# Layer-norm tiles of 32 rows from each quarter of a group of 512

## The chip, the core and the metric

The kernel runs on one core of one Trainium2 chip. A core has five engines, each with its own queue of instructions in a fixed order: TensorE (PE) for matmuls, VectorE (DVE) and ScalarE (ACT) for elementwise work, GpSimd (POOL) for elementwise work and for issuing some DMA transfers, and SyncE (SP), which here only issues DMA transfers. Engines wait for one another through semaphores. Sixteen DMA engines move the data. The metric is the device time of one execution in microseconds (us).

## What is computed

The input x has 2 batches of 1,024 tokens with 512 features. Four blocks follow one another, each adding its result to x:

```python
x = x + attn_a(layernorm(x))     # gated linear attention, 4 heads, chunks of 128 tokens, a state per head
x = x + ffn(layernorm(x))        # silu(gate) * up, down; integer weights with scales, 1408 hidden
x = x + attn_b(layernorm(x))     # softmax attention over the 1,024 tokens of a batch
x = x + ffn(layernorm(x))        # the same ffn again

def layernorm(x, eps=1e-05):
    m = mean(x, axis=-1); v = var(x, axis=-1)
    return (x - m) / sqrt(v + eps)
```

A layer norm works on each token by itself. What follows it is a product over the 512 features, so the normed tile is needed turned, with features on the partitions and tokens along the row.

## The kernel before

The 2,048 tokens are 16 tiles of 128 rows (`NT`). Four tiles (`ST`) are a group of 512, and there are four groups (`NST`). The stages are called a (first attention), f (first ffn), b (second attention) and g (second ffn). Between the stages x lies in DRAM, as x1 behind a, x2 behind f and x3 behind b, each as 16 tensors of 128 rows. x1 is stored at L680 and x2 at L931.

Matrices are kept as a high and a low part, and a product is made of three matmuls (L89, L90, L91) or, in the f and g stages and for the scores of b, as seven products of combined 2x2 blocks instead of eight (L338, L1023). ACT makes the high part (L75), DVE the low one (L76). Nearly all of TensorE's time goes to these.

The layer norm of 14 of the 16 group norms goes the way that the change touches: groups 2 and 3 of a, and all four groups of f, b and g. (Groups 0 and 1 of a are turned by TensorE, `ln_tile`, L130.) `ln_steps` gives eight steps for a group, four of `ln_norm` and four of `ln_move`:

- `ln_norm` loads a tile of 128 rows to a buffer `xin` (L102, on SP; two buffers, and the next tile is asked for together with the present one), takes mean and variance on DVE (`bn`, L109, `mv`, L111), adds eps and takes the power -1/2 on POOL (`ve`, L113, `rs`, L115, and for a and f also L119), and writes the normed tile `xn`, on ACT for a and f (L120), on DVE for b and g (L122). DVE then turns it in blocks of 32x32 into `y` (L198), whose layout on a partition is (b, k, i, q): b for the block of 32 features within 128, k for the 128 features, i for the tile in the group, q for the token in its block of 32. There is one `y` buffer, so the next group's turn waits for the moves of this one.
- `ln_move` moves the blocks to the right partitions, to `xT` (L209): for each b and each c (block of 32 tokens in the tile) one DMA from 32 partitions to 32 partitions, 16 in a group. The token of a column of `xT` is 128 i + 32 c + q, so for given c a partition's data is 16 pieces of 32 floats: 128 bytes each, 512 pieces to a move. SP issues the moves of a and f, of b0, b1 and g3, and half of b2; POOL issues the others, 72 of 224.

Later steps split `xT` in high and low parts (`xh`, `xl`, `ln_split`) or combine two groups first (`combine`, L257).

Where these steps stand is set by two things. The program hands them out by tables (in a, the table `fill` gives the tile at which each step is written), and a scheduler then orders every engine's instructions by a timeline of its own, under the dependencies and under extra ones that the program states with `behind`. In a, `q_head` (L91, `pq`), `kv_tile` (`pWk`, `pWv`, evicted as `sWk`, `sWv` at L571), `k_norm` (squares at L588), `scores` (`pS`, L650, from `kT`, L624, and `qT`, L519) and `chunk_out` (`pl`, `pg`; `xra` at L669 and L677; the state at L644) run for one tile after another, with the decay rows (`row`, L534, L545) made by POOL and ACT. A dependency through a DRAM tensor goes by that tensor: a load waits for the stores to the tensor it reads.

Of the kernel before, what the change touches and what calls it, by code (L numbers as in the profile page):

```python
# [9 lines left out]
F32 = mybir.dt.float32  # L10
# [6 lines left out]
P = 128  # L17
D = 512
# [3 lines left out]
NT = NB * T // P  # L22
# [3 lines left out]
ST = 4  # L26
NST = NT // ST
# [7 lines left out]
def hybrid_block_kernel(ctx: ExitStack, tc: tile.TileContext, a, out):  # L35
    nc = tc.nc
# [7 lines left out]
    dp = ctx.enter_context(tc.tile_pool(name="dram", bufs=1, space=bass.MemoryType.DRAM))  # L44
# [55 lines left out]
    def load_x(src, name, tag="xin"):  # L100
        xin = (rp if tag == "xres" else xp).tile([P, D], F32, tag=tag, name=f"xin_{name}")
        nc.sync.dma_start(out=xin, in_=src)  # L102
        return xin
# [31 lines left out]

    bq_s, sg_s, su_s = cols[:, 0:H], cols[:, H : H + KH], cols[:, H + KH : H + 2 * KH]

    x_in = a["x"]
    x1 = [dp.tile([P, D], F32, tag=f"x1_{t}", name=f"x1_{t}") for t in range(NT)]
    x2 = [dp.tile([P, D], F32, tag=f"x2_{t}", name=f"x2_{t}") for t in range(NT)]  # L140
    x3 = [dp.tile([P, D], F32, tag=f"x3_{t}", name=f"x3_{t}") for t in range(NT)]
    cl_d = [dp.tile([16, P], F32, tag=f"cl_{g}", name=f"cl_{g}") for g in range(NST)]
    p_d = [dp.tile([T // P, P, P], F32, tag=f"p_{i}", name=f"p_{i}") for i in range(NC)]
    vo_d = [dp.tile([P, 1024], F32, tag=f"vo_{k}", name=f"vo_{k}") for k in range(KD)]
# [41 lines left out]
    lnT, lnY, lnX, laid = {}, {}, {}, []  # L186

    def ln_norm(src, nm, st, i):


        t = st * ST + i
        for n in range(t, min(t + 2, st * ST + ST)):
            if (nm, n) not in lnX:
                lnX[nm, n] = load_x(src[n], f"{nm}{n}")
        if i == 0:
            lnY[nm, st] = yp.tile([P, 4, KD, ST, 32], F32, tag="y", name=f"y_{nm}{st}")
        xn = layernorm(lnX[nm, t], f"{nm}{t}", by_act=nm in "af")
        done = nc.vector.transpose(lnY[nm, st][:, :, :, i, :], xn.rearrange("p (k b q) -> p b k q", k=KD, b=4))  # L198
        laid[:] = [done.ins]

    def ln_move(nm, st, b):

        if b == 0:
            lnT[nm, st] = slot(f"xT_{nm}{st}").rearrange("p (k c) -> p k c", k=KD)
        y = lnY[nm, st]
        xf = lnT[nm, st].bitcast(F32).rearrange("p k (i b q) -> p (k i) b q", i=ST, b=4)
        for c in range(4):
            sync = nm in "af" or (nm, st) in (("b", 0), ("b", 1), ("g", 3)) or ((nm, st) == ("b", 2) and c % 2)
            (nc.sync if sync else nc.gpsimd).dma_start(  # L209
                out=xf[32 * b : 32 * (b + 1), :, c, :],  # L210
                in_=y[32 * c : 32 * (c + 1), b].rearrange("p k i q -> p (k i) q"),
            )

    def ln_split(nm, st):
# [10 lines left out]
    def ln_steps(src, nm, st):  # L225

        return [lambda i=i: ln_norm(src, nm, st, i) for i in range(ST)] + [
            lambda b=b: ln_move(nm, st, b) for b in range(4)
        ]
# [118 lines left out]
    with ExitStack() as actx:  # L348
# [11 lines left out]
            out=le, in_=ones, compare_op=ALU.is_ge, fill=0.0, base=0, pattern=[[1, P]], channel_multiplier=-1  # L360
# [9 lines left out]
        rows = a1.tile([P, 2 * D + 96], F32, name="rows")  # L370
# [38 lines left out]
                    done.extend(split(w[:, 0:512], w[:, 512:1024], staged[:, k]))  # L409
            return load if staged is None else done  # L410

        xa = [x_in[t * P : (t + 1) * P, :] for t in range(NT)]

        def ln_tile(t):
            st, i = divmod(t, ST)
# [315 lines left out]

        fill = [[] for _ in range(NT)]
        for src, nm, g, its in (
            (xa, "a", 2, (0, 0, 0, 1, 1, 1, 1, 1)),
            (xa, "a", 3, (2, 2, 3, 4, 4, 5, 5, 5)),
            (x1, "f", 0, (6, 6, 7, 7, 7, 7, 8, 8)),
            (x1, "f", 1, (9, 9, 10, 10, 10, 10, 11, 11)),
        ):
            for t, step in zip(its, ln_steps(src, nm, g)):
                fill[t].append(step)  # L740
# [6 lines left out]
        moving = combine("f", 0)  # L747
        wcs, loads = [], []
# [59 lines left out]
    def ffn(src, dst, nm, wcs, moving, ended, after):  # L808
# [3 lines left out]
        with ExitStack() as fctx:  # L812
# [5 lines left out]
            for pr in range(2):  # L818
# [90 lines left out]
                for i in range(2 * ST):  # L909
                    t = pr * 2 * ST + i  # L910
                    if 1 <= i < 2 * ST - 2:
                        n = i + 2
                        for js in (slice(0, 6), slice(6, KH)):
                            done = h_split(n, js, ha[:, n - 2, js] if n < ST else hb[:, n - ST, js], None)
                    xr = rp.tile([P, D], F32, tag="xres", name=f"xr{nm}{t}")
                    with behind((half,)):
                        nc.sync.dma_start(out=xr, in_=src[t])
                    o = fp.tile([P, 512], F32, tag="sg", name=f"o{nm}{t}")

                    last = nm == "g" and t == NT - 1  # L920
                    for ds in [slice(0, 256), slice(256, 512)] if last else [slice(0, 512)]:
                        ps = psum(f"po{nm}{t}_{ds.start}")[:, ds]
                        for j in range(KH):
                            nc.tensor.matmul(ps, hs[i][0][:, j], wd[j][:, ds], start=j == 0, stop=False)  # L924
                            nc.tensor.matmul(ps, hs[i][1][:, j], wd[j][:, ds], start=False, stop=j == KH - 1)  # L925
                        nc.vector.tensor_tensor(o[:, ds], ps, sd_b[:, ds], ALU.mult)
                        nc.vector.tensor_tensor(xr[:, ds], o[:, ds], xr[:, ds], ALU.add)
                        if last:
                            nc.sync.dma_start(out=dst[t][:, ds], in_=xr[:, ds])
                    if not last:  # L930
                        nc.sync.dma_start(out=dst[t], in_=xr)  # L931
                    with behind(done):
                        for _ in range((0, 3, 3, 2, 2, 2, 2, 0)[i]):
                            if early or late:
                                (early or late).pop(0)()
                    if pr == 0 and i in (3, 5, 6):
                        wcs.append(stationary(len(wcs), f"{nm}1", queue=nc.gpsimd))

    of_b = combine("b", 0)
    ffn(  # L940
        x1,
        x2,
        "f",
        wcs,
        moving,
        spilled,
        (ln_steps(x2, "b", 0) + ln_steps(x2, "b", 1), of_b[:6]),
    )


# [2 lines left out]
    with ExitStack() as bctx:  # L953
# [245 lines left out]
        wvo = blocks(vo_d, "wvo0_")  # L1199
        moving = of_b[6:]  # L1200
        for b in range(NB):
            nm, src, g = ("b", x2, 2) if b == 0 else ("g", x3, 0)
            norm = ln_steps(src, nm, g) + ln_steps(src, nm, g + 1)
            if b == 0:
                for kt in (4, 5, 6, 7):
                    array(v_tile, 0, kt)
                do(moving, 6)
                wm = blocks(m_d, "wm")
                do(norm, 8)
                for kt in range(4):  # L1210
                    array(v_tile, 0, kt)
                array(q_proj, 0, 0, range(KD))
            else:
                do(moving, 1)
                array(out_b, 0, 5)
                array(q_proj, 1, 0, range(KD))
                for i in (6, 7):
                    probs_split(0, i, last)
                do(moving, 4)
                array(out_b, 0, 6)  # L1220
                do(norm, 2)
                array(out_b, 0, 7)
                wvo = blocks(vo_d, "wvo1_")
                for kt in (4, 5, 6, 7):
                    array(v_tile, 1, kt)
                do(moving, 2)
                for kt in range(4):
                    array(v_tile, 1, kt)
                do(norm, 2)
                do(moving, 4)  # L1230
                do(norm, 4)
            q_operands(b, 0, False)
            q_operands(b, 0, True)
            if b == 0:
                do(norm, 2)
            cycle(b, 0, lambda: q_proj(b, 1, (0, 1)))
            for i in (0, 1):
                probs_T(b, i)
            do(norm, 2)
            cycle(b, 1, lambda: q_proj(b, 1, (2, 3)))  # L1240
            for i in (2, 3):
                probs_T(b, i)
            do(norm, 4 if b == 0 else 6)
            array(out_b, b, 0)
            if b:
                moving = combine("g", 0)
            cycle(b, 2, lambda: out_b(b, 1))
            for i in (4, 5):
                probs_T(b, i)
            array(out_b, b, 2)  # L1250
            if b == 0:
                moving = combine("b", 1)
                do(moving, 1)

            def between():
                out_b(b, 3)
                if b:
                    with behind(summed):
                        do(moving, 2)

            cycle(b, 3, between)
            if b == 0:
                for i in (6, 7):
                    probs_T(b, i)
                array(out_b, b, 4)
# [9 lines left out]
        ended = (array(out_b, 1, 7),)  # L1275

    out_t = [out[t * P : (t + 1) * P, :] for t in range(NT)]
    ffn(x3, out_t, "g", wcs, moving, ended, ([], []))


# [60 lines left out]
```

## Time and profile before

| | |
|---|---|
| runs | 927.61, 927.32, 926.01 us |
| median | 927.32 us |
| the profiled execution | 926.9 us |
| its span, from first to last instruction | 925.2 us |
| granted TensorE clock | 1.00 |
| DMA | 216,182 packets, 162.20 MB; 151,024 packets under 512 bytes |
| hardware queue (SP's transfers) | 212,624 packets, 53.7% of 16 engines' time |

The stages follow one another in time, with overlaps. Busy time in stretches of the span, in us:

| stretch | length | PE | DVE | ACT | POOL | DMA share |
|---|---|---|---|---|---|---|
| 0 to 100 (a) | 100 | 98.17 | 63.85 | 55.63 | 44.12 | 0.61 |
| 100 to 225 (a) | 125 | 124.60 | 83.40 | 70.75 | 60.62 | 0.61 |
| 225 to 420 (f) | 195 | 195.00 | 164.18 | 102.00 | 59.09 | 0.68 |
| 420 to 530 (f, b) | 110 | 110.00 | 86.80 | 44.62 | 25.10 | 0.56 |
| 530 to 690 (b) | 160 | 159.20 | 123.67 | 66.67 | 30.05 | 0.60 |
| 690 to 925 (g) | 235 | 231.49 | 168.53 | 94.23 | 38.44 | 0.48 |

A row of the groups in the profile reads: line, engine, operation, output<-input, count; then for one view the shortest, median and longest duration in ns, for another the start and duration in us with the idle time ahead of it and what ended it. A row "engine line <- engine line: a, n, c" says that the first waited for the second a us in all, n times, at most c us. The time from a DMA's issue to its landing is given apart from the time that the issue itself takes.

### The profile page before, as it was taken

What the parts mean: (1) busy time and instruction counts of PE and PEld (TensorE: products, weight loads), DVE (VectorE), ACT (ScalarE), POOL (GpSimd) and SP (SyncE); (2) the same over time, 40 slices, a digit from 0 to 9 for tenths busy, and PEclk for the clock granted to TensorE, in tenths of its full rate; (3) what the DMA queues carried; (4) which work ended last, traced back from release to release, by engine and by line L of the source; (5) the groups of instructions that cost most, each with busy time, mean ns of one, the idle gap of its engine ahead of it and who ended that gap; (6) DMA issues with size and microseconds to landing.
All of it is one profiled execution on the core that took longest, in us unless ns stands there. A gap on an engine that the chain in (4) does not pass through costs nothing.

```text
span 925.2 us, 13659 instructions
## 1 busy us (share of the span) xinstructions
PE 918.5 (99%) x4546; PEld 778.1 (84%) x4546; DVE 690.4 (75%) x1335; ACT 433.9 (47%) x928; POOL 257.4 (28%) x458
## 2 busy tenths in 40 slices
PE   9999999999999999999999999999999999999998
PEld 7899999998888888888888888888878888888887
DVE  6755657479998798778848878569968886967654
ACT  5645365556776334444234444145434444344431
POOL 4345334557563002211130401140501631001100
PEclk9999999999999999999999999999999999999999
DMA  9535655477979754724733769225969735454022
GB/s 304 210 100 124 208 160 152 158 207 262 367 236 321 214 178 153 216 47 150 281 82 83 171 168 261 69 45 137 239 140 369 259 126 137 165 205 138 22 69 80
DMA packets 216182, 162.20 MB, mean 175 GB/s; under 512 B 151024, under 2 KB 167728, under 8 KB 216112
## 3 DMA queue, kind: packets, MB, share of 16 engines
q1 hardware_dynamic: 212624, 150.05, 53.7%
q0 software_dynamic: 3488, 11.28, 4.5%
q8 instruction: 36, 0.59, 0.3%
q14 instruction: 34, 0.28, 0.1%
HBM read 104.76 MB, written 41.84 MB: 158 GB/s over the span
## 4 chain that ended last, share of the span: by engine, by line
PE 94%; DVE 2%; SPq 1%; DMA 1%; issue 1%; ACT 0%; POOL 0%; DVEq 0%; ACTq 0%
PE pXf L338 4%; PE pog L925 4%; PE pog L924 4%; PE pZf L338 4%; PE pof L925 4%; PE pXg L338 4%; PE pVg L338 4%; PE pVf L338 4%; PE pZg L338 4%; PE pof L924 4%; PE pob L91 3%; PE pob L89 3%; PE pob L90 3%; PE psZ L1023 2%; PE psX L1023 2%; PE psV L1023 2%
## 5 line engine op out<-in xcount | busy, mean ns | idle before, releaser
L924 PE MATMUL pog<-wdg,hsg 128*128 128x512 f32 (+1 forms) x165 | 60.1, 375 | 0.0
L925 PE MATMUL pog<-wdg,hsg 128*128 128x512 f32 (+1 forms) x165 | 60.0, 375 | 0.0
L925 PE MATMUL pof<-wdf,hsf 128*128 128x512 f32 x154 | 59.1, 389 | 0.0
L924 PE MATMUL pof<-wdf,hsf 128*128 128x512 f32 x154 | 58.9, 389 | 0.0
L91 PE MATMUL pob<-vh,ptl 128*128 128x512 f32 x128 | 49.9, 390 | 0.8 <-DVE ptl L76 0.8
L89 PE MATMUL pob<-vh,pth 128*128 128x512 f32 x128 | 49.9, 390 | 0.0
L90 PE MATMUL pob<-vl,pth 128*128 128x512 f32 x128 | 49.8, 389 | 0.0
L76 POOL TENSOR_TENSOR hsg<-sgg,hsg 128x128 fp32r<-128x128 f32 x40 | 18.9, 491 | 110.4 <-ACT hsg L75 102.6
L338 PE MATMUL pXg<-B_g,wcg 128*128 128x512 f32 x176 | 46.2, 389 | 0.0
L338 PE MATMUL pVf<-T_f,wcf 128*128 128x512 f32 x176 | 46.2, 389 | 0.0
L338 PE MATMUL pVg<-T_g,wcg 128*128 128x512 f32 x176 | 46.2, 389 | 0.0
L338 PE MATMUL pXf<-B_f,wcf 128*128 128x512 f32 x176 | 45.9, 390 | 0.0
L113 POOL TENSOR_SCALAR ve_g<-mv_g 128x1 f32<-128x1 f32 x16 | 7.7, 486 | 129.6 <-DVE mv_g L111 129.6
L209 POOL DMA_DIRECT2D xT_g<-y_g x48 | 31.1, 655 | 38.5 <-DVE T_b L76 29.2
L338 PEld LDWEIGHTS pXf<-B_f,wcf 128*128 128x128 f32 x176 | 32.9, 188 | 7.1 <-issue 0.3
L338 PEld LDWEIGHTS pVf<-T_f,wcf 128*128 128x128 f32 x176 | 33.0, 188 | 6.9
L338 PEld LDWEIGHTS pVg<-T_g,wcg 128*128 128x128 f32 x176 | 33.0, 188 | 6.9
L338 PEld LDWEIGHTS pXg<-B_g,wcg 128*128 128x128 f32 x176 | 33.0, 188 | 6.9
L545 ACT ACTIVATE row<-row,ncl 128x128 f32<-128x128 f32 x64 | 20.5, 391 | 35.4 <-POOL row L534 35.4
L113 POOL TENSOR_SCALAR ve_b<-mv_b 128x1 f32<-128x1 f32 x16 | 5.7, 359 | 112.4 <-DVE mv_b L111 112.2
L924 PEld LDWEIGHTS pog<-wdg,hsg 128*128 128x128 f32 x165 | 31.1, 188 | 5.7
L925 PEld LDWEIGHTS pog<-wdg,hsg 128*128 128x128 f32 x165 | 31.0, 188 | 5.6
(344 smaller groups left out, 2837.4 us busy)
## 6 DMA issues: line engine op xcount, KB each, us to landing
wcg<-wc SPq DMA_DIRECT2D x19, 896.0 KB, 5.0
wc<-wcf SPq DMA_DIRECT2D x11, 896.0 KB, 5.8
p<-py SPq DMA_DIRECT2D x15, 512.0 KB, 3.5
wcf<-wc SPq DMA_DIRECT2D x8, 896.0 KB, 6.3
ptl<-p SPq DMA_DIRECT2D x56, 128.0 KB, 3.1
xin_a<-in_x SPq DMA_DIRECT2D x16, 256.0 KB, 5.3
xra<-in_x SPq DMA_DIRECT2D x16, 256.0 KB, 3.4
row<-cl SPq DMA_DIRECT2D x16, 256.0 KB, 4.3
```

Of the source, the lines that this page charges most:

```text
L76: return c.ins, (eng or nc.vector).tensor_tensor(lo, src, hi.bitcast(F32), ALU.subtract).ins
L89: nc.tensor.matmul(ps, lhs_hi, rhs_hi, start=first, stop=False)
L90: nc.tensor.matmul(ps, lhs_hi, rhs_lo, start=False, stop=False)
L91: end = nc.tensor.matmul(ps, lhs_lo, rhs_hi, start=False, stop=last).ins
L113: nc.gpsimd.tensor_scalar(ve, mv[:, 1:2], EPS, None, ALU.add)
L209: (nc.sync if sync else nc.gpsimd).dma_start(out=xf[32 * b : 32 * (b + 1), :, c, :], in_=y[32 * c : 32 * (c + 1), b].rearrange("p k i q -> ...
L338: nc.tensor.matmul(ps, w[:, m, k * P : (k + 1) * P], o[:, s, k, :], start=first and k == 0 and s == 0, stop=k == 1 and s == 1, skip_group_ ...
L545: nc.scalar.activation(row[:, h, :], row[:, h, :], AF.Exp, bias=ncl[:, n : n + 1], scale=-1.0)
L924: nc.tensor.matmul(ps, hs[i][0][:, j], wd[j][:, ds], start=j == 0, stop=False)
L925: nc.tensor.matmul(ps, hs[i][1][:, j], wd[j][:, ds], start=False, stop=j == KH - 1)
L1023: ends[nm] = nc.tensor.matmul(ps, o[:, i, k], w[:, j, k], start=first and k == 0 and i + j == 0, stop=k == 1 and i == 1, skip_group_check= ...
```

## The change

x1, x2 and x3 become four tensors of 512 rows each; `in_tiles` gives the old tiles of 128 rows as slices of them, for the stores and for the residual loads. A layer-norm tile i of a group is no longer rows 128 i to 128 i + 127, but 32 rows from each quarter: rows 128 c + 32 i + q for c from 0 to 3. It is loaded by one DMA with four pieces of 32 rows; each row still is 2 KB and goes to one partition. Then block c of tile i holds tokens 128 c + 32 i + q, so that for given c the (i, q) of `y` are 128 tokens in a row, and a move has 4 pieces of 128 floats on each partition: 512 bytes, 128 pieces to a move. The columns of `xT` are in the same order as before, and what follows is the same. A load now reads rows of all four tiles of its group, where before it read one.

```diff
+    def in_tiles(groups):
+        return [x[i * P : (i + 1) * P, :] for x in groups for i in range(ST)]
+
     x_in = a["x"]
-    x1 = [dp.tile([P, D], F32, tag=f"x1_{t}", name=f"x1_{t}") for t in range(NT)]
-    x2 = [dp.tile([P, D], F32, tag=f"x2_{t}", name=f"x2_{t}") for t in range(NT)]
-    x3 = [dp.tile([P, D], F32, tag=f"x3_{t}", name=f"x3_{t}") for t in range(NT)]
+    x1_g = [dp.tile([ST * P, D], F32, tag=f"x1_{g}", name=f"x1_{g}") for g in range(NST)]
+    x1 = in_tiles(x1_g)
...
         for n in range(t, min(t + 2, st * ST + ST)):
             if (nm, n) not in lnX:
-                lnX[nm, n] = load_x(src[n], f"{nm}{n}")
+                rows = src[st].rearrange("(c i q) d -> i c q d", c=4, i=ST)
+                lnX[nm, n] = load_x(rows[n - st * ST], f"{nm}{n}")
...
-        xf = lnT[nm, st].bitcast(F32).rearrange("p k (i b q) -> p (k i) b q", i=ST, b=4)
+        xf = lnT[nm, st].bitcast(F32)
         for c in range(4):
             sync = nm in "af" or (nm, st) in (("b", 0), ("b", 1), ("g", 3)) or ((nm, st) == ("b", 2) and c % 2)
             (nc.sync if sync else nc.gpsimd).dma_start(
-                out=xf[32 * b : 32 * (b + 1), :, c, :],
-                in_=y[32 * c : 32 * (c + 1), b].rearrange("p k i q -> p (k i) q"),
+                out=xf[32 * b : 32 * (b + 1), :, c * P : (c + 1) * P],
+                in_=y[32 * c : 32 * (c + 1), b].rearrange("p k i q -> p k (i q)"),
             )
...
-        xa = [x_in[t * P : (t + 1) * P, :] for t in range(NT)]
+        x_g = [x_in[g * ST * P : (g + 1) * ST * P, :] for g in range(NST)]
+        xa = in_tiles(x_g)
...
-            (xa, "a", 2, (0, 0, 0, 1, 1, 1, 1, 1)),
-            (xa, "a", 3, (2, 2, 3, 4, 4, 5, 5, 5)),
-            (x1, "f", 0, (6, 6, 7, 7, 7, 7, 8, 8)),
-            (x1, "f", 1, (9, 9, 10, 10, 10, 10, 11, 11)),
+            (x_g, "a", 2, (0, 0, 0, 1, 1, 1, 1, 1)),
+            (x_g, "a", 3, (2, 2, 3, 4, 4, 5, 5, 5)),
+            (x1_g, "f", 0, (6, 6, 7, 7, 7, 7, 8, 8)),
+            (x1_g, "f", 1, (9, 9, 10, 10, 10, 10, 11, 11)),
...
                     with behind((half,)):
-                        nc.sync.dma_start(out=xr, in_=src[t])
+                        nc.sync.dma_start(out=xr, in_=in_tiles(src)[t])
```

x2 and x3 are made in the same way, and the calls of `ffn` and `ln_steps` hand over the lists of groups (`x1_g`, `x2_g`, `x3_g`). The lines of the changed kernel stand 9 or 10 below those of the kernel before: L209 becomes L218, L198 becomes L207, L571 becomes L581. The number of instructions on every engine stays the same; the scheduler gives some of them another place.

More of the change, by code (lines that the diff above doesn't have):

```diff
@@ L136, in hybrid_block_kernel @@
     bq_s, sg_s, su_s = cols[:, 0:H], cols[:, H : H + KH], cols[:, H + KH : H + 2 * KH]
+    def in_tiles(groups):
+        return [x[i * P : (i + 1) * P, :] for x in groups for i in range(ST)]
     x_in = a["x"]
-    x1 = [dp.tile([P, D], F32, tag=f"x1_{t}", name=f"x1_{t}") for t in range(NT)]
-    x2 = [dp.tile([P, D], F32, tag=f"x2_{t}", name=f"x2_{t}") for t in range(NT)]
-    x3 = [dp.tile([P, D], F32, tag=f"x3_{t}", name=f"x3_{t}") for t in range(NT)]
+    x1_g = [dp.tile([ST * P, D], F32, tag=f"x1_{g}", name=f"x1_{g}") for g in range(NST)]
+    x1 = in_tiles(x1_g)
+    x2_g = [dp.tile([ST * P, D], F32, tag=f"x2_{g}", name=f"x2_{g}") for g in range(NST)]
+    x2 = in_tiles(x2_g)
+    x3_g = [dp.tile([ST * P, D], F32, tag=f"x3_{g}", name=f"x3_{g}") for g in range(NST)]
+    x3 = in_tiles(x3_g)
     cl_d = [dp.tile([16, P], F32, tag=f"cl_{g}", name=f"cl_{g}") for g in range(NST)]
@@ L940, in hybrid_block_kernel @@
     ffn(
-        x1,
+        x1_g,
         x2,
@@ L946, in hybrid_block_kernel @@
         spilled,
-        (ln_steps(x2, "b", 0) + ln_steps(x2, "b", 1), of_b[:6]),
+        (ln_steps(x2_g, "b", 0) + ln_steps(x2_g, "b", 1), of_b[:6]),
     )
@@ L1201, in hybrid_block_kernel @@
         for b in range(NB):
-            nm, src, g = ("b", x2, 2) if b == 0 else ("g", x3, 0)
+            nm, src, g = ("b", x2_g, 2) if b == 0 else ("g", x3_g, 0)
             norm = ln_steps(src, nm, g) + ln_steps(src, nm, g + 1)
@@ L1277, in hybrid_block_kernel @@
     out_t = [out[t * P : (t + 1) * P, :] for t in range(NT)]
-    ffn(x3, out_t, "g", wcs, moving, ended, ([], []))
+    ffn(x3_g, out_t, "g", wcs, moving, ended, ([], []))
 def _layouts(i):
```

## The prediction

> **What bounds the kernel now.** I read the busy table first, then the waits of TensorE.
>
> ```profile
> PE 918.5 (99%) x4546; PEld 778.1 (84%) x4546; DVE 690.4 (75%) x1335; ACT 433.9 (47%) x928; POOL 257.4 (28%) x458
> ```
>
> ```profile
> PE warm L685 <- POOL ones L356: 1.3, 1, 1.3
> PE pob L91 <- DVE ptl L76: 0.8, 1, 0.8
> PE pxT_a L130 <- DVE xn_a L122: 0.5, 1, 0.5
> PE pS L650 <- ACT kT L624: 0.4, 1, 0.4
> ```
>
> TensorE idles 925.2 − 918.5 = 6.7 us, 1.3 + 0.5 us of it at the start, most of the rest after the last matmuls. The granted clock is 1.00. So other engines matter only through lateness that reaches a matmul, and a gain is small at best: in the middle only the waits of 0.8 us (at 684.4) and 0.4 us (at 99.9) are open, and from matmul start to matmul start they cost 0.97 and 0.56 us, 1.5 us together. What can be lost has no such limit, so I then read the places where a wait for a layer-norm load comes close to a matmul. The first, from the timeline (start, duration, idle before and its releaser):
>
> ```profile
> 60.12 6.03 SPq L102 DMA_DIRECT2D xin_a<-in_x  x3
> 62.66 0.69 DVE L109 BATCH_NORM_STATS2 bn_a<-xin_a 128x6 f32<-128x512 f32 x1 [0.73 <-DMA xin_a<-in_x]
> ...
> 63.42 0.17 DVE L111 BATCH_NORM_AGGREGATE mv_a<-bn_a 128x2 f32<-128x6 f32 x1
> ...
> 63.68 0.23 POOL L113 TENSOR_SCALAR ve_a<-mv_a 128x1 f32<-128x1 f32 x1 [4.20 <-DVE mv_a L111]
> ...
> 64.97 0.81 ACT L120 ACTIVATE xn_a<-xin_a,mv_a,rs_a 128x512 f32<-128x512 f32 x1 [1.30 <-POOL mv_a L119]
> 65.69 0.56 ACT L624 COPY kT<-pkT 128x512 f32<-128x512 f32 x1
> ...
> 66.58 0.61 PE L650 MATMUL pS<-qT,kT 128*128 128x128 f32 x4
> ```
>
> The load issued at 60.12 releases DVE at 62.66. Statistics, POOL's inverse root and ACT's xn follow with no gap worth a name, kT stands behind xn on ACT and ends at 66.26, and pS needs it at 66.58: 0.32 us to spare. The second place:
>
> ```profile
> 135.34 0.69 DVE L109 BATCH_NORM_STATS2 bn_f<-xin_f 128x6 f32<-128x512 f32 x1 [1.21 <-DMA xin_f<-x]
> ...
> 136.17 0.66 DVE L571 TENSOR_TENSOR sWk<-pWk,rows 128x512 f32<-128x512 f32 x1
> 139.91 0.69 DVE L109 BATCH_NORM_STATS2 bn_f<-xin_f 128x6 f32<-128x512 f32 x1 [3.09 <-DMA xin_f<-x]
> ...
> 139.15 2.17 ACT L75 CAST xh_a<-xT_a 128x512 fp32r<-128x512 f32 x4
> ```
>
> DVE idles 1.21 and 3.09 us for two loads, and pq's matmuls at 139.84 and 145.27 follow their inputs by 0.08 and 0.12 us.
>
> **The change, part by part.** *Moves.* 224 moves (14 groups of 16) go from 512 pieces of 128 bytes to 128 of 512. The rows for one issue, and the nearest with 128 pieces:
>
> ```profile
> L209 SPq DMA_DIRECT2D xT_a<-y_a x32: 597/627/1716, 75.4 to 120.8; - x32
> L102 SPq DMA_DIRECT2D xin_f<-x x16: 319/320/1277, 100.2 to 278.6; - x16
> ```
>
> SP issues 152 moves and POOL 72. On SP one falls from 0.627 towards 0.32 us, so a group's 16 from about 11.5 to 5.3 us; 152 × 0.3 = 46 us of SP are freed. Nearly all of it is hidden, because TensorE runs meanwhile. It counts at 99.9 us: the moves of a2, issued 75.4 to 87.3, end DVE's 2.4 us wait before y_a at 88.9, and lateness runs on through the decay rows and xn_a to kT. With the last move landing some 5 us earlier, that stall goes: −0.5 us.
>
> *Group loads.* A load now reads rows of four tiles, so it waits for the group's fourth store. In the changed order xin_f0, issued at 100.2 before, stands behind the store of x1_3: xra done near 103.2, store landed 2.3 us later, load issued near 105.7. Behind it on SP are an xra load, xin_f1 (which waits for ACT until 108.5 anyway) and a3's moves, which would start near 112 instead of 109.5 and end before 118 instead of at 121.5. Who wants them is ACT at 139: no cost. In the f and b stages the loads move likewise, and pvb's last matmul at 469.9, which gates the b2 moves, gives them over 10 us of cover; without that cover each late load would hold DVE for its 2.5 us.
>
> *Scheduling order.* No instruction is added or removed on the compute engines, but some change places. Near 220 us DVE makes a low half of V2 (L76, 0.73 us) behind those of T2_f and T3_f (1.75 us each) instead of ahead of them, so it ends near 223.5 instead of at 220.41, about when pV's matmuls with it begin (222.3, with 1.9 to spare before): 0 to +0.65 by what the order drops ahead of it, I take +0.3, the middle. Near 684 an xT_g subtraction of 1.2 us stands before the softmax maxima, into 0.6 us of idle time: +0.1 to +0.4, I take +0.2. Elsewhere I found no moved instruction that takes more than its matmul has to spare.
>
> *How a load is spread.* This decides. 56 of the 64 loads at L102 ask no longer for 128 consecutive rows but for 4 pieces of 32. No row shows a transfer whose outermost count is 4; those here begin with 128, 32 or 16. Low end: still dealt out as before, 2.5 us to landing unhindered, cost 0. High end: four shares, one for each piece, on 4 engines. Its price comes from the DMA view of 60 to 64 us, which holds two loads and little else:
>
> ```profile
> DMA packets 288, 0.52 MB, mean 131 GB/s; under 512 B 32, under 2 KB 32, under 8 KB 288
> q1 hardware_dynamic: 288, 0.52, 47.1%
> ```
>
> 16 engines × 4 us × 0.471 / 288 = 0.105 us per packet. Eight packets on each engine become 32, so 24 × 0.105 = +2.5 us to landing. [...]
>
> [...]
>
> Five places pay when a load lands 2.5 us later:
> 1. Near 36 us: xin_a9 (issued 30.31) lands at 35.3 and its statistics began at 33.35, so DVE is held 2.0 us. Behind stands xn_a7, with 1.05 us to spare at the transposes: +0.9.
> 2. At 66.6: 2.5 − 0.32 = +2.2.
> 3. Near 88: bn at 77.21 holds state, then POOL's unbroken chain from 78.6 to 85.5, xn_a and kT. pS has 1.77 to spare: +0.7.
> 4. At 135 to 146: sWk ends at 139.3 instead of 136.8, four squares on ACT (1.2 us) follow, so the xh_a casts start 1.4 late: +1.3 at 139.84. The second load holds xT_a's low half 2.5 us, of which 0.12 is spare: +1.1 more.
> 5. Near 188: bn at 176.39 holds state and POOL, 1.9 to spare: +0.6.
>
> Sum: 0.9 + 2.2 + 0.7 + 2.4 + 0.6 = 6.8; with −0.5 + 0.3 + 0.2 it stays 6.8. The profiled execution took 926.9 us (span 925.2 and 1.7 around it), 0.4 below the median of 927.32. 926.9 + 6.8 = 933.7, and I say **933.5**. With the low end the sum is 926.9.
>
> **The rivals.**
> - *Loads spread as before.* Then faster moves are hidden and the new places cost little: 926.9, between 925.5 (neither middle wait left: −1.5) and 928.5 (both reorderings at their upper ends and some noise). For it: nothing but the pattern of the load changes. Against: that pattern has four pieces.
> - *Faster.* Both middle waits go and no stall comes: 926.9 − 1.5 = 925.4. The waits of 0.4 and 0.8 speak for it; at 684 nothing near that wait gets earlier.
> - *Slower through order alone.* From 200 to 300 us DVE is busy 22 to 23.4 of every 25 us. If the order there costs one eviction 2 to 4 us and TensorE has 0.75 to 1 us to spare (243 to 250 us), the price is 1 to 3: 928 to 930. It decides once DVE has no idle time left to catch up.
> - *The moves do not get cheaper*, because issue does not go by pieces: −0.5 falls away, and the loads still pay: 934.2.
>
> **How the numbers follow.** Late loads 0.72 (range 929.5 to 939), order alone 0.06, loads as before 0.17, faster 0.05; the moves' rival lies within the first. The upper end takes pairs of loads in one queue (0.8 us apart, up to 1.7 us more for the second) and the f loads at 245 to 285 us, where DMA is 0.80 to 0.94 busy. Range 927.5 to 938.5; without the rival of unchanged loads it would be 929.5 to 938.5. A measurement of this kernel tells 0.2% (1.9 us) from no change; so faster 0.05, same 0.17, slower 0.78.
>
> **What would show it.** Right: xin landing above 4.5 us where it was 2.5, the wait of DVE's bn for DMA growing from 14.5 us on the f tiles, pS waiting for kT by about 2 us near 66 and pq for xh_a near 140, moves at 0.33 us on SP, TensorE idle near 13 us. Wrong: landing still at 2.5 with idle time near 6.7.

## The result and the profile after

The changed kernel takes 988.98 us (median of 4 runs, 988.04 to 989.90) beside 927.47 us for the kernel before on the same chip: a ratio of 1.0666, 95% interval 1.0647 to 1.0684. The forecast was 933.5 us, so the sign was right and the size was not: +61.5 us measured, +6.8 worked out.

The first lines to read are again the busy table and the chain that ended last, here from the page of the changed kernel.

```profile
PE 936.0 (95%) x4546; PEld 785.0 (80%) x4546; DVE 691.5 (70%) x1335; ACT 434.4 (44%) x928; POOL 244.7 (25%) x458
...
DMA packets 157142, 162.19 MB, mean 164 GB/s; under 512 B 72528, under 2 KB 108688, under 8 KB 157072
...
PE 58%; DMA 22%; DVE 7%; POOL 4%; SPq 3%; ACT 3%; issue 3%; DVEq 0%; ACTq 0%; POOLq 0%
```

The span is 986.3 us. TensorE idles 986.3 − 936.0 = 50.3 us of it, where it idled 6.7. Its matmuls, the same 4,546, also take 936.0 − 918.5 = 17.5 us longer. 43.6 + 17.5 = 61.1 us is the whole growth of the span. DMA holds 22% of the chain, where TensorE held 94% and DMA 1% before. The packets fell from 216,182 to 157,142, all of it among SP's transfers; POOL's queue has 3,488 as before.

The longest waits of TensorE (total, times, longest, in us), where none was above 1.3 us before:

```profile
PE pS L660 <- ACT kT L634: 10.8, 6, 3.3
PE psY L1033 <- ACT opS L75: 8.5, 1, 8.5
PE pob L91 <- DVE ptl L76: 4.7, 2, 3.9
PE pZg L347 <- DVE pZg L889: 3.0, 1, 3.0
```

They are many and spread over all stages, and the releaser named is the last link only. One step further back, the waits of DVE in the changed kernel:

```profile
DVE bn_f L109 <- DMA xin_f<-x: 38.4, 14, 8.5
...
DVE bn_g L109 <- DMA xin_g<-x: 22.3, 10, 5.8
DVE bn_a L109 <- DMA xin_a<-in_x: 19.8, 7, 5.0
...
DVE bn_b L109 <- DMA xin_b<-x: 11.2, 5, 3.2
DVE y_b L207 <- DMA xT_b<-y_b: 10.4, 1, 10.4
```

The four rows of `bn` sum to 91.7 us. The same four in the kernel before were 14.5, 1.2, 3.6 and 0.8: 20.1 us. So the statistics of a layer norm wait for its load, 36 times instead of 15.

Why the loads are late shows best where little else moves. The DMA view of 60 to 72 us has 40 slices of 0.3 us; a digit is the busy share of the 16 DMA engines in tenths. The kernel before:

```profile
DMA  0002989776400000000000378999329900099200
GB/s 0 0 0 89 307 266 253 143 232 253 164 34 7 0 0 0 0 0 0 0 0 0 96 150 314 348 341 389 109 82 416 369 7 0 14 382 410 68 0 0
```

The changed kernel, whose loads are issued at 61.92 and 62.75:

```profile
DMA  0100000000062011222222222222222000000004
GB/s 0 55 0 0 0 0 0 0 0 0 7 55 20 14 34 75 102 96 102 109 102 96 102 109 102 96 102 109 102 96 89 27 0 0 0 0 0 0 0 34
```

Before, the first burst is two loads of 256 KB, drained in nine slices at up to 307 GB/s. After, the digit stands at 2 for 15 slices at about 100 GB/s; over 65 to 69 us the share is 0.26, as with 4 engines of 16 at work and 12 idle. The completion records agree. The load issued at 61.92 has one update at 0.99 us and four from 5.15 to 5.38; the same load before had sixteen, the last at 2.52. The second load of the pair goes through the same four engines, the digit still at 2 with both under way, and lands after 7.13 us. The packets under 512 bytes tell the same: 8 for the two loads here, where two loads before had 32 (60 to 64 us). So 4 engines of the 16 served a load.

Over all 56 loads of L102 that the change touches, from issue to the last of the load's own updates:

| kernel | pieces in a load | shortest, us | median, us | longest, us |
|---|---|---|---|---|
| before | 128 rows in a row | 2.51 | 3.65 | 8.53 |
| changed | 4 | 5.31 | 7.32 | 12.82 |

The moves, by the source view of their line (minimum/median/maximum ns of one issue):

```profile
L218 SPq DMA_DIRECT2D xT_f<-y_f x64: 585/599/1739, 161.1 to 341.0; - x64
L218 POOL DMA_DIRECT2D xT_g<-y_g x48: 548/548/633, 666.1 to 800.5; - x48
...
L218 SPq DMA_DIRECT2D xT_a<-y_a x32: 586/600/1713, 80.8 to 133.7; - x32
```

A fourth of the pieces costs SP 0.600 us instead of 0.627, and POOL 0.548 instead of 0.648.

Stretches of 50 us of the changed kernel (length, busy us of each engine with its instructions, granted clock, DMA share, GB/s) show where TensorE's time goes:

```profile
150.00:200.00 50.00, 44.87 (x283) 40.16 (x282) 23.63 (x67) 23.93 (x70) 17.46 (x33) 0.97 0.40 124
200.00:250.00 50.00, 41.85 (x286) 37.67 (x285) 40.12 (x84) 26.66 (x76) 27.61 (x41) 0.97 0.59 202
250.00:300.00 50.00, 49.97 (x223) 41.15 (x223) 40.20 (x79) 31.90 (x58) 30.18 (x47) 0.96 0.76 274
300.00:350.00 50.00, 44.93 (x188) 35.73 (x187) 34.75 (x70) 26.78 (x51) 14.01 (x24) 0.97 0.73 237
...
500.00:550.00 50.00, 41.53 (x177) 33.90 (x176) 26.57 (x59) 14.90 (x34) 7.38 (x16) 0.93 0.22 64
```

TensorE idles 10.5 us up to 150 (2.2 before), 5.1 from 150 to 200, 13.3 from 200 to 350, 8.5 from 500 to 550, 3.9 from 600 to 650, 5.4 from 700 to 850, and 3.7 at the end as before: 50.3 together, of which 30 us more than before lie behind 200 us. The granted clock falls below 1.00 in the four stretches from 150 to 350 us and in those that begin at 500, 600 and 750; in the kernel before it did so in none.

The longest stall shows both, the idle time and the clock. In the timeline of the changed kernel (start, duration, idle before and its releaser):

```profile
503.67 11.80 SPq L102 DMA_DIRECT2D xin_b<-x  x4
515.53 10.08 SPq L218 DMA_DIRECT2D xT_b<-y_b  x8
...
527.75 1.30 DVE L207 STREAM_TRANSPOSE y_b<-xn_b 128x512 f32<-128x512 f32 x2 [10.40 <-DMA xT_b<-y_b]
...
530.65 1.22 PE L1033 MATMUL psY<-T_b,opS 128*128 128x512 f32 x2 [8.47 <-ACT opS L75]
```

The last loads of the group are issued at 514.20 and 514.97 and land 7.27 and 10.04 us later. The eight moves that SP issues behind them took 5.74 us before and take 10.08 now: SP itself waits for `xin_b` there (4.8 us in two times between 500 and 532). The next group's turn into `y` needs the moves landed, and the matmul starves 8.47 us. In windows of 1 us (length, TensorE busy, granted clock, DMA share, GB/s):

```profile
522.00:523.00 1.00, 0.17 (x1) 1.00 0.40 134
...
526.00:527.00 1.00, 0.00 (x0) 0.98 0.25 66
527.00:528.00 1.00, 0.00 (x0) 0.50 0.00 0
...
530.00:531.00 1.00, 0.35 (x1) 0.50 0.03 8
...
533.00:534.00 1.00, 1.00 (x4) 0.61 0.00 0
534.00:535.00 1.00, 1.00 (x6) 1.00 0.00 0
```

The clock halves at about 526.96, 4.8 us after the last matmul ended, and stays halved for 3.1 us after the next began at 530.65. It does not take so long a stall. Around the one of 2.47 us that ends at 184.95 (same columns):

```profile
183.00:184.00 1.00, 0.00 (x0) 1.00 0.27 102
184.00:185.00 1.00, 0.05 (x1) 1.00 0.21 80
185.00:186.00 1.00, 1.00 (x4) 0.81 0.01 2
186.00:187.00 1.00, 1.00 (x4) 0.50 0.00 0
...
189.00:190.00 1.00, 1.00 (x9) 0.98 0.12 37
```

The clock falls four more times in this profile, at stalls of 2.8 to 3.9 us (ending at 249.35, 317.49, 631.92 and 792.89), and not at one of 2.56 us (70.96). Where the clock falls, a stall is paid twice: the matmuls behind it run at 0.50 for 3.1 to 4.7 us.

### The profile page after: what moved, and what is told of

It is laid out like the page before. It is cut to its first block, busy times and chain, and to the rows that moved or that the text cites. A ratio compares the mean times of both kernels' runs of the same rounds, so it can differ in the third digit from the quotient of the medians.

```text
span 986.3 us, 13660 instructions
## 1 busy us (share of the span) xinstructions
PE 936.0 (95%) x4546; PEld 785.0 (80%) x4546; DVE 691.5 (70%) x1335; ACT 434.4 (44%) x928; POOL 244.7 (25%) x458
## 2 busy tenths in 40 slices
DMA packets 157142, 162.19 MB, mean 164 GB/s; under 512 B 72528, under 2 KB 108688, under 8 KB 157072
## 3 DMA queue, kind: packets, MB, share of 16 engines
q0 software_dynamic: 3488, 11.28, 3.8%
## 4 chain that ended last, share of the span: by engine, by line
PE 58%; DMA 22%; DVE 7%; POOL 4%; SPq 3%; ACT 3%; issue 3%; DVEq 0%; ACTq 0%; POOLq 0%
DMA xin_f<-x 4%; PE pog L935 4%; PE pog L934 4%; DMA xin_b<-x 4%; DMA xin_a<-in_x 4%; DMA xin_g<-x 3%; PE pZf L347 3%; PE pVg L347 3%; PE pZg L347 3%; PE pXf L347 3%; PE pXg L347 3%; PE pVf L347 3%; PE pof L935 3%; PE pof L934 3%; PE pob L91 2%
## 5 line engine op out<-in xcount | busy, mean ns | idle before, releaser
L109 DVE BATCH_NORM_STATS2 bn_f<-xin_f 128x6 f32<-128x512 f32 x16 | 11.0, 693 | 38.4 <-DMA xin_f<-x 38.4
L218 POOL DMA_DIRECT2D xT_g<-y_g x48 | 26.3, 554 | 41.2 <-DVE T_b L76 27.4
L113 POOL TENSOR_SCALAR ve_b<-mv_b 128x1 f32<-128x1 f32 x16 | 3.5, 228 | 132.0 <-DVE mv_b L111 131.9
L934 PEld LDWEIGHTS pog<-wdg,hsg 128*128 128x128 f32 x165 | 31.1, 188 | 5.7
```

Source lines behind the costliest of these rows:

```text
L109: nc.vector.bn_stats(bn, xin)
L113: nc.gpsimd.tensor_scalar(ve, mv[:, 1:2], EPS, None, ALU.add)
L218: (nc.sync if sync else nc.gpsimd).dma_start(out=xf[32 * b : 32 * (b + 1), :, c * P : (c + 1) * P], in_=y[32 * c : 32 * (c + 1), b].rearra ...
```

## The experiments

The leading theory: a load in 4 pieces is served by 4 engines, and that alone makes the loss. Rivals: the new order and the wait for a whole group make it; the 512-byte moves have a share; or the loads' lateness matters less than what their requests do to others, and then by SP's queue or by the shared engines.

### One change of count: 16 and 8 pieces instead of 4

The changed kernel with every load read in 16 pieces of 8 rows, or 8 of 16. Moves keep 512 bytes; the blocks of `y` are laid out as (k, b, token). The two have the same instructions in the same order.

```diff
-                rows = src[st].rearrange("(c i q) d -> i c q d", c=4, i=ST)
+                rows = src[st].rearrange("(c i q) d -> i c q d", c=16, i=ST)   # 8 in the other
...
-            lnY[nm, st] = yp.tile([P, 4, KD, ST, 32], F32, ...)
+            lnY[nm, st] = yp.tile([P, KD, 4, P], F32, ...)
...
-        done = nc.vector.transpose(lnY[nm, st][:, :, :, i, :], ...)
+        y = lnY[nm, st].rearrange("p k b (a i q) -> p (k b) a i q", a=4, i=ST)   # a=2 in the other
+        done = nc.vector.transpose(y[:, :, :, i, :], xn.rearrange("p (n a q) -> p n a q", n=4 * KD, a=4))
...
-                in_=y[32 * c : 32 * (c + 1), b].rearrange("p k i q -> p k (i q)"),
+                in_=y[32 * c : 32 * (c + 1), :, b],
```

> The changed kernel, but a layer-norm tile takes 8 rows from each sixteenth of its group: a load has 16 pieces of 8 rows, still one request, still rows of all four tiles, and the moves still have pieces of 512 bytes. Theory (a load in 4 pieces is served by 4 of the 16 DMA engines, and that is nearly all of the loss): the loads land in 2.2 to 2.8 us again when nothing else runs, 926 to 935 us. Rival (the wait for all four stores of a group and the new order of instructions cost the time): 980 to 990 us, as the changed kernel.

> The same with 8 pieces of 16 rows, the order of instructions as in the one with 16 pieces. Theory: 8 engines, landing near 3.2 us when nothing else runs (a third of the way from 2.4 to 5.2), 930 to 950 us. Rival: 980 to 990 us, no difference from 16 or 4 pieces.

Later the same layout with 4 pieces closed the row:

> The changed kernel with the blocks laid out as in the 16- and 8-piece versions, so that the three differ in the number of pieces alone. If the number of engines of a load sets the time, 975 to 995 us, as the change itself; if the way in which the transposes write their blocks has a part in it, it lies clearly below, at 960 or less.

| pieces | time, us | ratio to before | interval | TensorE busy, us | landing, us (shortest, median, longest) |
|---|---|---|---|---|---|
| 16 | 931.35 | 1.0040 | 1.0025 to 1.0055 | 919.9 | 3.17, 3.85, 8.76 |
| 8 | 943.06 | 1.0164 | 1.0149 to 1.0179 | 924.4 | 3.92, 4.96, 10.57 |
| 4 | 990.1 | 1.0672 | 1.0649 to 1.0694 | 941.1 | 5.35, 7.22, 12.82 |

The number of pieces makes the loss, and it grows faster than the landing does: 0.8 us on the shortest landing from 16 to 8 costs 11.7 us, 1.4 us more from 8 to 4 costs 47. Both shortest landings are above their forecasts (2.2 to 2.8, and near 3.2), while the times lie within theirs. The way in which the transposes write has no part that shows, since 990.1 is the time of the change itself within its interval. Order, group wait and 512-byte moves, all of which the version with 16 pieces has, cost 3.6 us together (2.3 to 5.1 by the interval), with the price of the 16 pieces themselves.

The late loads are the smaller part of what is late. From the version with 16 pieces to that with 4, whose instructions stand in the same order, the 64 loads of L102 together take 173 us more from issue to landing, and the other 623 transfers 349 us more.

### The count alone, in the kernel before

The kernel before, with its own order and moves, but each load reading its 128 rows in 4 or in 16 pieces. The rows come in another order within the tile, so the tokens of the output are permuted.

```diff
-                lnX[nm, n] = load_x(src[n], f"{nm}{n}")
+                lnX[nm, n] = load_x(src[n].rearrange("(q c) d -> c q d", c=4), f"{nm}{n}")   # 16 in the other
```

> The kernel before, with a tensor for each tile and the moves of 128-byte pieces, but each layer-norm load of groups 2 and 3 of a and of f, b and g takes the 128 rows of its tile in 4 pieces (every fourth row), so that tokens of a tile come out in another order. No wait for the group. Theory: the loads land in 5.2 us or later and the time is 965 to 995 us. Rival: 926 to 935 us.

> The same with 16 pieces of 8 rows (every sixteenth row), in the same order of instructions. It tells the number of engines from the mere shape of the request, whose issue took 0.52 instead of 0.32 us in the changed kernel. Theory: 926 to 931 us. If the shape of the request costs the time: the same as with 4 pieces.

With 4 pieces 983.95 us, ratio 1.0586 (1.0548 to 1.0623); with 16 pieces 930.23, 1.0022 (1.0012 to 1.0032). Every instruction has the same place in both. So 53.7 us come from the count, with nothing else of the change present. A load of 16 pieces has its own small price: its shortest landing is 3.16 us, 0.65 above that of 128 rows in a row. The version of the change with 16 pieces is at 1.0040 and this at 1.0022, with intervals that overlap: what is left for order, group wait and moves can't be told from nothing.

### The moves of 512 bytes alone

The changed kernel, loads of 128 consecutive rows, moves of 512 bytes. The tokens are permuted within a group.

```diff
-                rows = src[st].rearrange("(c i q) d -> i c q d", c=4, i=ST)
-                lnX[nm, n] = load_x(rows[n - st * ST], f"{nm}{n}")
+                lnX[nm, n] = load_x(in_tiles(src)[n], f"{nm}{n}")
```

> The changed kernel with one part undone: a layer-norm load takes the 128 consecutive rows of its tile as before, so that it waits for one store; tensors of 512 rows and moves of 512-byte pieces stay, and the tokens of a group come out in another order. Theory (all loss lies in the loads): 925.5 to 929 us, and since SP's issue of a move took 0.60 us with 128 pieces and 0.63 with 512, the moves gain nothing that shows. Rival (faster moves are worth something by themselves): below 925.5 us.

926.75 us, ratio 0.9995 (0.9985 to 1.0004): no gain that can be told from none. The waits of TensorE keep their place (columns as above):

```profile
PE pS L659 <- ACT kT L633: 1.0, 1, 1.0
PE pob L91 <- DVE ptl L76: 0.8, 1, 0.8
```

Both middle waits of the kernel before are still there, and the moves take SP 0.599 us each (median of `xT_f`). The loads keep about the places that they had before (the first f load is issued at 101.02; before at 100.22, with the change at 115.47), so this run says nothing on the wait for a whole group.

### Four requests in place of one

The changed kernel, each load as four requests of 32 consecutive rows.

```diff
+        if len(src.shape) == 3:
+            for c in range(4):
+                nc.sync.dma_start(out=xin[32 * c : 32 * (c + 1)], in_=src[c])
+            return xin
```

> The changed kernel with each load as four requests of 32 rows, whose outermost count is 32. Theory (16 engines for each): landing in 2.2 to 3 us when nothing else runs, 927 to 935 us in spite of 168 more requests on SP, each about 0.32 us. Rival (the four pieces, the wait for the group or the order cost the time): above 960 us.

940.92 us, ratio 1.0152 (1.0121 to 1.0183). It wins back most of the loss, and all 16 engines serve each request (16 updates), but it misses its forecast of 927 to 935 and stays 9.6 us above the version with 16 pieces in one request. Whether the 168 more requests on SP or the other order of instructions make the rest is not shown.

### Does the late load hurt, or the queue that it leaves?

The kernel before with its loads untouched, and behind each of the 56 one more request for the same rows into a DRAM tile that nobody reads, in 4 pieces or in 16. The two have the same instructions in the same order.

```diff
-        nc.sync.dma_start(out=xin, in_=src)
+        asked[:] = [nc.sync.dma_start(out=xin, in_=src).ins]
...
+                more = dp.tile([P, D], F32, tag=f"more_{nm}{n}", name=f"more_{nm}{n}")
+                with behind(asked):
+                    nc.sync.dma_start(out=more, in_=src[n].rearrange("(q c) d -> c q d", c=4))   # 16 in the other
```

> The kernel before, whole and with its fast loads; right behind each layer-norm load of the changed kind (56) SP issues one more request of 4 pieces of 32 rows, which copies the same tile to a DRAM tensor of its own that nothing reads. No instruction waits for its data. Theory Q (a slow request does its harm in the queue: SP waits for the eighth request before, and four DMA engines hold up the others' pieces): 945 to 980 us, far above the twin with 16 pieces. Theory L (the harm is the lateness of the layer-norm tile itself, for which DVE stands still): within 1% of the twin, 928 to 940 us.

> The twin: the same order of instructions, but the 56 further requests have 16 pieces of 8 rows. Both theories: 928 to 940 us, the cost of 56 more requests of 256 KB.

965.73 us, ratio 1.0412 (1.0395 to 1.0430), beside 933.69, 1.0067 (1.0050 to 1.0084). The 32 us between them are lost to requests whose data nobody reads. The DMA view of 615 to 624 us, in slices of 0.225 us, of the kernel with 4 pieces, where a g load is issued at 615.30 and the unread request at 615.67:

```profile
DMA  9643226989522222222222222499722222894985
GB/s 382 237 164 128 100 109 200 291 291 391 210 109 100 100 100 100 109 100 100 91 109 100 109 91 100 164 410 419 291 109 100 109 100 91 173 191 146 391 310 200
```

And of its twin from 585 to 594 us, the same load issued at 585.43:

```profile
DMA  6222114948969860000000000069920000675899
GB/s 264 109 109 82 73 73 164 200 137 328 328 264 382 337 246 9 0 0 0 0 0 0 0 0 0 0 255 410 410 91 0 0 0 0 73 109 191 346 382 419
```

The burst of 256 KB and its unread copy are over at once in the twin; with 4 pieces a tail of twos at 100 GB/s follows for 14 slices. Whatever is issued into that tail has its shares on the four busy engines served late. The load itself, on 16 engines, shows it: twelve of its sixteen updates come at 2.27 to 2.46 us and four at 4.73 to 5.27, where in the twin all sixteen come at 2.12 to 2.65. Over the 56 loads the median landing is 5.08 us against 3.81. In all, the 64 loads take 40 us more to land than in the twin, and the 623 transfers that are neither loads nor unread requests 289 us more.

### By SP's queue, or by the engines?

SP's requests share eight completion semaphores in turn (75 or 76 of its 605 requests on each, in both kernels), and in the changed kernel SP waited 30.4 us for `xin` loads, where it had waited 4.2 us before. To tell this from the shared engines, the unread requests went to POOL's queue, where they hold no semaphore of SP.

```diff
-                    nc.sync.dma_start(out=more, in_=src[n].rearrange("(q c) d -> c q d", c=4))
+                    nc.gpsimd.dma_start(out=more, in_=src[n].rearrange("(q c) d -> c q d", c=4))   # 16 in the other
```

> Before, plus 56 unread requests of 4 pieces, as in the earlier pair, but put on POOL's queue instead of SP's. If what hurts is that SP itself waits for slow requests (each of SP's requests waits for the eighth before it), then a slow request on POOL's queue holds up nothing on SP, and this kernel should be within 8 us of its twin with 16 pieces. If what hurts is that the pieces of the kernel's own transfers queue on the same four DMA engines, the queue that asked makes no difference: 20 to 35 us slower than the twin, and the kernel's own loads that follow such a request show 12 landings of their 16 at the usual 2.3 to 2.7 us and 4 near 5.

> The twin: the same unread requests on POOL's queue, in 16 pieces, with the same instructions in the same order on every engine. By both theories a few us above before (930 to 945), for 56 more issues on POOL and 14.7 MB more traffic. Its own time is no test; the difference from the 4-piece kernel is.

992.55 us, ratio 1.0709 (1.0689 to 1.0730), beside 955.33, 1.0305 (1.0282 to 1.0328). The twin missed its forecast of 930 to 945. Ahead of an unread request POOL waits, in order with its other work, for the stores of x: 226 us in all in the twin and 252 with 4 pieces (rows of `more_f`, `more_b` and `more_g`). Between the two lie 37.2 us, above the 20 to 35 of the second theory and far above the 8 of the first. Of POOL itself only one wait is for such a request to land:

```profile
POOL xT_b L213 <- DMA more_b<-x: 2.2, 1, 2.2
```

13 of the 64 layer-norm loads show the pattern of twelve early updates and four more than 0.5 us later (4 in the twin, none in the kernel before), and the 623 other transfers take 203 us more to land than in the twin. So slow requests do their harm without holding a semaphore of SP, and shares on the engines are seen to come late. But 37.2 us is no clean price of the shared engines, because on POOL's queue the two kernels differ in more. The queue's packets, MB and share, with 4 pieces and with 16:

```profile
q0 software_dynamic: 18720, 26.05, 9.4%
q0 software_dynamic: 7968, 25.96, 9.1%
```

The 10,752 packets more have some 8 bytes each (0.09 MB together). One issue takes POOL about 0.16 us longer with 4 pieces (`more_g` 0.689 us against 0.522, medians), 9 us over the 56, and POOL's longer waits for the stores (252 against 226 us) may carry the lateness on. What SP's own waits add in the changed kernel has no run of its own; it is not shown to be nothing.

## Why the prediction was right and wrong

- **What bounds the kernel**: right. TensorE's waits before held 1.5 us to win, and losses had no limit.
- **Moves cheaper on SP** (0.627 towards 0.32 us, −0.5 us at 99.9): wrong. They cost 0.600. The row that I took as nearest, a plain load with 128 pieces, shared the count of pieces with the new move and not its shape; the loads of the change, in 4 pieces, went the other way, from 0.32 to 0.555 us (median of `xin_f`). The rival "the moves do not get cheaper" was right in this, and with 512-byte moves alone the kernel gains nothing (0.9995): the wait of `pS` that was to go grows from 0.4 to 1.0 us.
- **Group loads and order** (0, +0.3 and +0.2): about right. With 16 pieces all that is in; the first f load is issued at 106.1 (forecast 105.7), `pV` waits 0.2 us for V's low half, and the wait of 0.8 us of `pob` stays as it was. The kernel is 3.6 us slower, 2.5 of which (930.23 against 927.72) the request's shape takes by itself in the kernel before.
- **How a load is spread, high end**: right in kind, 4 engines. No trace of the kernel before shows that four pieces go to 4 engines: the high end was my estimate, and the changed kernel shows it, with four late updates at 5.15 to 5.38 us. The price of +2.5 us was the size for a lone load in a quiet place: measured +2.8 on the shortest landing. It was wrong as the price of all 56: the median grows by 3.7 us and the longest is 12.82. The loads come in pairs, the second waits for the first on the same four engines (7.13 us), and transfers on all 16 engines leave a share there.
- **Five places pay** (6.8 us): this is the step that failed. I took one load at a time, put its lateness against the slack of the place, left all other transfers as they were, and put everything outside these places at nothing. The places themselves came, but for the second part of the fourth (+1.1), which is not there at 157.79:

```profile
38.74 0.33 PE L130 MATMUL pxT_a<-ident,xn_a 128*128 128x128 f32 x1 [1.22 <-DVE xn_a L122]
70.96 0.38 PE L660 MATMUL pS<-qT,kT 128*128 128x128 f32 x1 [2.56 <-ACT kT L634]
95.66 0.38 PE L660 MATMUL pS<-qT,kT 128*128 128x128 f32 x1 [1.59 <-ACT kT L634]
152.32 0.50 PE L89 MATMUL pq<-xh_a,Wq 128*128 128x512 f32 x1 [2.09 <-ACT xh_a L75]
209.23 0.38 PE L660 MATMUL pS<-qT,kT 128*128 128x128 f32 x1 [1.59 <-ACT kT L634]
```

That is 9.1 us against 6.8. TensorE's idle time grew by 43.6, so 34.5 us were lost in places for which I had nothing, some 27 of them behind 210 us. At the longest of these the load itself was hidden and what stood behind it was not: eight moves, then `y`, then 8.47 us of TensorE. The runs show why: transfers that the change does not touch come late (349 us more in all, beside 173 for the loads), and 56 unread requests of 4 pieces cost 32 us on SP's queue, by twins with the same instructions in the same order. An estimate by difference, 53.7 for loads in 4 pieces less 32, leaves some 22 us for the loads' own lateness, if the two add up. No run shows that part by itself, and the unread requests are copies to DRAM that come on top of the loads.
- **No term for the clock**: missing. The matmuls took 17.5 us longer. The granted clock short of 1.00, summed over the stretches of 50 us, makes about 13 us, a part of it in idle time; the remainder I can't assign.
- **The signs to look for**: landing above 4.5 us, a growing wait of `bn_f` (38.4), `pS` waiting for `kT` (2.56 us where about 2 near 66 was named) and `pq` for `xh_a` came; moves at 0.33 us and TensorE idle near 13 us did not.

The range (927.5 to 938.5) failed with the sum: its upper end took the second load of a pair to be 1.7 us later, and never asked what a quarter of the engines does to the transfers that were not changed.

No version here beats the kernel before. Of those that keep the order of the tokens, the one with 16 pieces comes closest, at 1.0040.

## What to carry to other kernels

When an edit changes the outermost count of a DMA, read how many engines serve it (the digits of the DMA view in a quiet window, the completion updates of one request) before costing anything else. Counts of 16, 32 and 128 got all 16 engines here (16 updates of a request), a count of 4 got four. A request on few engines is not only late itself: it stands in the way of the transfers that have a share on those engines (56 unread requests in 4 pieces cost 32 us more than in 16), so its price lies also in what is queued behind it, and not in the slack of its own reader alone. When stalls may reach some 2.5 us on TensorE, add a term for the clock: it fell here at one of 2.47 us, though not at one of 2.56.

## What the runs showed of the hardware

- Engines serving a load: with 128 rows, 16, 8 and 4 pieces of the same 256 KB, the shortest landing is 2.51, 3.17, 3.92 and 5.31 us. With 16, 8 and 4 pieces the pages count 73,200, 72,752 and 72,528 packets under 512 bytes: over 56 loads 8 fewer and then 4 fewer to a load, which fits 16, 8 and 4 engines. From 8 to 4 pieces, 16 more packets on an engine take 1.4 us: an estimate of 0.087 us for one of 2 KB.
- Issue on SP goes more by the request's shape than by its pieces: 0.627 us for 512 pieces and 0.600 for 128 of a move, 0.32 for a plain load, and for one of three dimensions 0.52 to 0.56 in 4 pieces, 0.59 to 0.63 in 8 and 0.53 to 0.54 in 16 (medians by stage).
- The clock fell to 0.50 at six stalls of TensorE, the shortest of 2.47 us, and came back 3.1 to 4.7 us after the next matmul began; a stall of 2.56 us did not bring it down.
